# Graph layer on one core: each strip of node features is loaded where it is normalised, into two buffers, in place of two strips ahead into three

## The chip, the core and the metric

The kernel runs on one NeuronCore of a Trainium2 chip. The metric is device time of one launch in microseconds (us), the median of several runs; three runs of the kernel before gave 2588.91, 2590.05 and 2590.2 us, so the median is 2590.05 us. One execution was also recorded by the hardware profiler; everything called "the trace" or "the profile" below is that execution.

The engines are PE (matrix products), DVE (vector work), ACT (activation functions and copies), POOL (here almost only indirect DMAs) and SP (issues of DMAs). Each takes its instructions strictly in the order in which the program gives them. DMAs are issued by SP, ACT and POOL and are carried out by 16 DMA engines that all issuers share.

## What is computed

One layer of a graph network over 12,500 nodes with 64 features and 212,500 edges sorted by destination:

```
h = relu(layernorm(x))                        # 12500 x 64
edge_in = concat([h[src], h[dst], weight])    # 212500 x 129
e = silu(silu(edge_in @ eW1 + eb1) @ eW2 + eb2)
agg = segment_sum(e, src, 12500)              # 12500 x 128
out = x + silu(concat([h, agg]) @ nW1 + nb1) @ nW2 + nb2
```

## The kernel before

The product of `edge_in` with `eW1` is split: the part of `h[src]` and the part of `h[dst]` are products of nodes, made once for each node and written to two tables in DRAM, `ta` and `tb`.

**Strips.** Node number n belongs to bucket n mod 100; there are 100 buckets of 125 nodes. The node features are taken in strips of 12 buckets (`CH` = 12): eight strips of 12 and a ninth of 4, numbered 0 to 8 here. A strip goes through three steps. It is loaded into a buffer `xs` of 128 x 12 x 64 (function `loaded`, two DMAs of SP on line 570, one for 112 partitions and one for 13). It is normalised in place by `norm`, called by `normed`: DVE sums it (L532, L533) and centres it (L535), ACT squares (L536), DVE sums the squares (L539, L540), ACT takes the root (L541), DVE inverts and scales (L543, L544). Then `products` handles four buckets at a time: PE turns them (L551) and multiplies (L180), ACT copies out (L555, L183, L591, L597), DVE splits the rows into three bf16 parts (L593, L599), and SP writes the results to `hd`, `tb` and `ta` (L586, L594, L601).

**Blocks.** The edges are taken in 208 blocks of 1024. For a block s, `count` makes a one-hot of the edges' buckets (L306, L307), a running count by a scan in three pieces (L317) and a product (L322). `send` takes the rank of each edge from PE (L341), makes destination rows `to` on DVE (L361), the products of the `tb` window with PE (L349), copies them to `qs` on ACT (L356, L365), and POOL scatters them with eight indirect DMAs (L370) into a queue `q` in DRAM. SP loads what a block needs: `bc` and `bb` (L265, L267), the window `win` (L281) and the edge weights `pick` (L292). There are 11 chunks of blocks, each with a queue; while one chunk is sent, ACT issues the fills of the next chunk's queue with zeros (L100, up to 1.6 MB in one DMA).

**Steps.** When a chunk is sent, its queue is read back (`qt`, L415, with rows of `ta`, `a`, L420), and a pipeline of steps (L438 to L516) finishes the edges and adds them up by bucket. Steps of chunk c run among the sends of chunk c+1.

**Order.** PE, DVE, ACT and SP run in the order in which the program emits instructions. The strips' work is a generator, `feed`, that is advanced a few pieces at a time between the pieces of `send_all`: four at each piece while chunk 0 is sent and for some pieces after it, then two at each hook of the steps' loop. `groups` makes the list of the strips' pieces, and `turns` keeps up to three of them going in turn, one piece of each in a round. In the kernel before, strips 0 and 1 are loaded first, then strip 0 is normalised; from then on strip i+2 is loaded ahead of the products of strip i, and strip i+1 is normalised after the first products of strip i. With three buffers strip i uses buffer i mod 3.

Of the kernel before, what the change touches and what calls it, by code (L numbers as in the profile page):

```python
# [28 lines left out]
F32 = mybir.dt.float32  # L29
# [9 lines left out]
P = 128  # L39
# [7 lines left out]
G = 4  # L47
# [12 lines left out]
def tile_gnn(ctx: ExitStack, tc: tile.TileContext, x, src, dst, ew, eW1, eb1, eW2, eb2, nW1, nb1, nW2, nb2, out):  # L60
    nc = tc.nc
    N, D = x.shape
# [44 lines left out]
    CH = 12  # L107
# [64 lines left out]
    def product(s, hr, ps, tag, to):  # L172

        abs_ = []
        for a in range(2):

            half = slice(a * D, (a + 1) * D)
            ab = ps.tile([P, G // 2, H], F32, name="ab", tag=tag)
            for i in range(G // 2):
                nc.tensor.matmul(ab[:, i], hr[half, i, :], w1[half, s, :], start=True, stop=True)  # L180
            abs_.append(ab)
        for a in range(2):
            nc.scalar.copy(to.rearrange("l (i a) h -> l a i h", a=2)[:, a], abs_[a])  # L183
# [7 lines left out]
    for win in wins:  # L191
        nc.vector.memset(win, 0.0)
        for a in range(2):
            for i, row in enumerate((w1d, eb1b)):
                at = a * HB + WL + i
# [43 lines left out]
    with ExitStack() as work:  # L239
# [287 lines left out]
        def norm(xs, n):  # L527

            xs = xs[:, :n, :]
            wide = [P, n, D]  # L530
            mean = fp.tile([P, NE], F32, name="mean")[:, :n]
            nc.vector.tensor_reduce(mean, xs, AX.X, OP.add)  # L532
            nc.vector.tensor_scalar(mean, mean, 1.0 / D, None, op0=OP.mult)  # L533
            cen = fp1.tile([P, NE, D], F32, name="cen")[:, :n]
            nc.vector.tensor_tensor(cen, xs, mean[:, :, None].to_broadcast(wide), op=OP.subtract)  # L535
            nc.scalar.activation(xs, cen, AF.Square)  # L536
            yield
            var = fp.tile([P, NE], F32, name="var")[:, :n]
            nc.vector.tensor_reduce(var, xs, AX.X, OP.add)  # L539
            nc.vector.tensor_scalar(var, var, 1.0 / D, EPS, op0=OP.mult, op1=OP.add)  # L540
            nc.scalar.activation(var, var, AF.Sqrt)  # L541
            yield
            nc.vector.reciprocal(var, var)  # L543
            nc.vector.scalar_tensor_tensor(xs, cen, 0.0, var[:, :, None].to_broadcast(wide), op0=OP.max, op1=OP.mult)  # L544
            yield

        def turned(xs, g):

            ht = mm.tile([P, G // 2, P], F32, name="ht", tag="mm")
            for i in range(G // 2):  # L550
                nc.tensor.transpose(  # L551
                    ht[:, i, :], xs[:, g + 2 * i : g + 2 * i + 2, :].rearrange("p j d -> p (j d)"), ident
                )
            hr = fp.tile([P, G // 2, P], F32, name="hr")
            nc.scalar.copy(hr, ht)  # L555
            return hr
# [8 lines left out]
            nc.sync.dma_start(tb0.rearrange("(p j) f -> p j f", j=NE)[:, g : g + G, :], got)  # L565
            yield

        def loaded(b0, n, xs):
            for part_ in (slice(0, 112), slice(112, L)):
                nc.sync.dma_start(xs[part_, :n, :], x_rows[part_, b0 : b0 + n, :])  # L570
            yield

        def normed(b0, n, xs):
            yield from norm(xs, n)
            yield
            ready.add(b0)

        def products(b0, g, xs):

            assert b0 in ready  # L580
            b = b0 + g
            hr = turned(xs, g)
            yield
            rows_a = fp.tile([P, G, H], F32, name="rows_a")
            product(0, hr, mm, "mm", rows_a)
            nc.sync.dma_start(hd[:, b // 2 : (b + G) // 2, :], hr)  # L586
            yield
            got = fp.tile([P, G, H], F32, name="got")
            product(1, hr, mm, "mm", got)
            parts = fp.tile([P, G, 3, H], BF16, name="parts")  # L590
            nc.scalar.copy(parts[:, :, 0, :], rows_a)  # L591
            yield
            nc.vector.tensor_tensor(rows_a, rows_a, parts[:, :, 0, :], op=OP.subtract)  # L593
            nc.sync.dma_start(tb_buckets[:, b : b + G, :], got)  # L594
            done_b.append(b // G)
            yield
            nc.scalar.copy(parts[:, :, 1, :], rows_a)  # L597
            yield
            nc.vector.tensor_tensor(parts[:, :, 2, :], rows_a, parts[:, :, 1, :], op=OP.subtract)  # L599
            yield  # L600
            nc.sync.dma_start(ta_buckets[:, b : b + G, :], parts.rearrange("p b s f -> p b (s f)"))  # L601
            done_a.append(b // G)
            yield
# [84 lines left out]
        def groups():  # L688

            starts = list(range(0, NB, CH))  # L690
            size = lambda b0: min(CH, NB - b0)
            of = [(b0, size(b0), xss[i % len(xss)]) for i, b0 in enumerate(starts)]
            todo = [loaded(*of[0]), loaded(*of[1]), normed(*of[0])]
            for i, b0 in enumerate(starts):
                if i + 2 < len(starts):
                    todo.append((b0, loaded(*of[i + 2])))
                todo += [(b0, products(b0, g, of[i][2])) for g in range(0, size(b0), G)]
                if i + 1 < len(starts):
                    todo.insert(len(todo) - size(b0) // G + 1, normed(*of[i + 1]))
            return todo  # L700

        done_a, done_b, ready = [], [], set()
        feeding = ExitStack()
        fp = feeding.enter_context(tc.tile_pool(name="fp", bufs=3, side="right"))
        fp1 = feeding.enter_context(tc.tile_pool(name="fp1", bufs=1, side="right"))
        xss = [fp1.tile([P, CH, D], F32, name=f"xs{i}") for i in range(3)]
        for xs in xss:
            nc.gpsimd.memset(xs, 0.0)

# [2 lines left out]
        with tc.tile_pool(name="lists", bufs=1, side="right") as lp:  # L712
# [4 lines left out]
            f, sf, t = (lp.tile([NP, PAIR], F32, name=n) for n in ("f", "sf", "t"))  # L717
# [25 lines left out]
            for _ in counting:  # L743
                pass
            feed = itertools.chain(checks(), turns(groups(), 3))
            for _ in send_all(0):
                for _ in range(4):
# [30 lines left out]
        at = 0  # L778
        for k in range(first, len(steps) + 2):
            for s in turn:  # L780
# [17 lines left out]
                else:  # L798
                    f, ahead = s
# [152 lines left out]
```

## Time and profile before

| quantity | value |
|---|---|
| median of three runs | 2590.05 us |
| the profiled execution, time and span | 2590.2 us, 2588.4 us |
| PE, DVE, ACT, POOL busy, share of the span | 85%, 79%, 48%, 67% |
| mean granted clock of PE | 0.926 |
| first and last indirect DMA of POOL (1661 of them) | 63.7 us, ended 2340.1 us |
| loads of strips (L570), first and last issue | 64.9 us, 246.9 us |
| sums of strips (L532), first and last start | 77.2 us, 290.8 us |
| fills of the second and third queue that lie among them, issue | 62.45, 91.49, 102.61, 152.59, 165.93, 184.05 and 202.49 us |

Times in the trace count from the start of the span. The strips are handled in the first eighth of the span, while chunks 0 and 1 are sent. "Busy" for POOL counts the execution of an indirect DMA and not the time of some 0.3 us between two of them, which the profile names "issue". What a wait is put down to is inferred by the profile from the semaphore that came last.

### The profile page before, as it was taken

The numbers are of one execution on the slowest core, as the hardware profiler recorded it, in microseconds if no ns is written. First come the engines' busy times: TensorE is split into PE (matmuls) and PEld (weight loads), VectorE is DVE, ScalarE is ACT, GpSimd is POOL, SyncE is SP. The second block draws the span as 40 slices with busy tenths as digits, with TensorE's granted clock in tenths as the row PEclk, the third lists the DMA queues.
The fourth block names the chain that finished last, engine by engine and source line by source line (L and its number), as shares of the span: only waits on it lengthen the run. The fifth ranks groups of instructions, "written<-read, shape, count | busy, mean of one in ns | idle before, by whom it ended". The sixth has DMA issues, their size and how long they took to land.

```text
span 2588.4 us, 60017 instructions
## 1 busy us (share of the span) xinstructions
PE 2205.0 (85%) x21814; PEld 2041.8 (79%) x21814; DVE 2034.8 (79%) x3464; ACT 1246.9 (48%) x2687; POOL 1736.8 (67%) x1729
## 2 busy tenths in 40 slices
PE   2456777988998998999899799889889999997997
PEld 1345667977987987888788799889879889996996
DVE  5877987987987887888788799879879889973442
ACT  2344634544554554555455455445545455553443
POOL 3675777777777777777677777777767777772000
PEclk7556888998999999999999899999989999998999
DMA  8787778669768767866966877786696667655441
GB/s 202 216 246 263 254 234 271 217 204 269 237 210 247 252 219 227 267 216 218 272 227 211 240 248 237 220 260 228 211 274 228 215 203 235 230 169 174 166 150 54
DMA packets 257977, 577.23 MB, mean 223 GB/s; under 512 B 51202, under 2 KB 110580, under 8 KB 257469
## 3 DMA queue, kind: packets, MB, share of 16 engines
q1 hardware_dynamic: 185096, 384.91, 45.7%
q0 software_dynamic: 54144, 123.04, 13.1%
q10 hardware_dynamic: 18434, 65.37, 11.4%
q8 instruction: 175, 2.87, 0.5%
q14 instruction: 128, 1.04, 0.1%
HBM read 361.44 MB, written 211.67 MB: 221 GB/s over the span
## 4 chain that ended last, share of the span: by engine, by line
PE 40%; DMA 23%; DVE 13%; POOL 7%; issue 6%; ACT 2%; SPq 1%; DVEq 0%; ACTq 0%; POOLq 0%
DMA q<-qs,to 14%; PE seg L505 10%; PE p L491 9%; POOL q L370 7%; PE pt L459 7%; PE pt L452 5%; DVE misc L317 5%; PE qp L349 4%; PE lr L438 3%; DMA bc<-rows 2%; DVE oneT L443 2%; DMA bb<-rows 2%; DVE one L472 2%; DMA pick<-in_edge_weight_dram 2%; DVE own L322 2%
## 5 line engine op out<-in xcount | busy, mean ns | idle before, releaser
L370 POOL DMA_INDIRECT q<-qs,to x1661 | 1697.4, 1022 | 602.7 <-issue 397.5
L463 ACT ACTIVATE e<-pt 128x512 f32<-128x512 f32 x525 | 313.7, 598 | 835.8 <-PE pt L459 769.6
L505 PE MATMUL seg<-one,e 128*128 128x125 f32 x4200 | 581.4, 282 | 54.7 <-DVE aggT L516 42.5
L491 PE MATMUL p<-w,e 128*128 128x128 f32 x4200 | 587.2, 284 | 5.3 <-ACT p L485 5.3
L317 DVE TENSOR_TENSOR_SCAN misc<-oh,misc 100x342 f32<-100x342 f16 (+1 forms) x623 | 579.7, 930 | 9.3 <-PE misc L341 1.2
L505 PEld LDWEIGHTS seg<-one,e 128*128 128x128 f32 x4200 | 524.4, 196 | 68.5 <-ACT p L485 27.7
L491 PEld LDWEIGHTS p<-w,e 128*128 128x128 f32 x4200 | 527.9, 197 | 31.0 <-issue 8.4
L443 DVE TENSOR_SCALAR oneT<-lr,part 125x512 bf16<-125x512 f32 x525 | 390.8, 744 | 111.1 <-PE lr L438 109.0
L459 PE MATMUL pt<-oneT,a 125*128 125x256 bf16 (+1 forms) x3300 | 443.0, 273 | 0.1
L452 PE MATMUL pt<-ident,qt 128*128 128x128 f32 x2100 | 332.0, 282 | 73.4 <-DVE oneT L443 73.4
L356 ACT COPY qs<-qp 128x512 f32<-128x512 f32 x416 | 229.2, 587 | 320.3 <-PE qp L349 225.7
L472 DVE TENSOR_TENSOR one<-nodes,qt 128x500 f32<-128x500 f32 x525 | 351.7, 670 | 0.7 <-PE seg L505 0.5
L459 PEld LDWEIGHTS <-a 125*128 125x128 bf16 x3300 | 318.7, 100 | 35.5 <-issue 1.0
L322 DVE TENSOR_TENSOR own<-misc,oh 100x342 f16<-100x342 f32 (+1 forms) x623 | 320.0, 514 | 21.6
L495 ACT ACTIVATE e<-p 128x512 f32<-128x512 f32 x525 | 314.1, 598 | 18.6 <-PE p L491 18.0
L485 ACT COPY p<-b2f 128x512 f32<-128x512 f32 x525 | 312.5, 595 | 0.1
L349 PE MATMUL qp<-win,pick 50*128 50x128 f32 x3322 | 260.7, 299 | 60.6 <-DMA pick<-in_edge_weight_dram 34.5
L349 PEld LDWEIGHTS qp<-win,pick 50*128 50x128 f32 x3322 | 220.4, 200 | 92.9 <-issue 71.5
L452 PEld LDWEIGHTS pt<-ident,qt 128*128 128x128 f32 x2100 | 228.3, 144 | 79.0 <-DVE oneT L443 76.3
L516 DVE TENSOR_TENSOR aggT<-aggT,seg 128x500 f32<-128x500 f32 x250 | 166.9, 667 | 94.2 <-PE seg L505 93.9
L438 PE MATMUL lr<-identb,qt 128*125 128x128 bf16 x2100 | 213.3, 225 | 30.6 <-DMA qt<-q 25.3
L438 PEld LDWEIGHTS <-qt 128*125 128x125 bf16 x2100 | 186.4, 139 | 42.1 <-DMA qt<-q 31.5
(121 smaller groups left out, 1086.3 us busy)
## 6 DMA issues: line engine op xcount, KB each, us to landing
qt<-q SPq DMA_DIRECT2D x250, 576.0 KB
a<-ta SPq DMA_DIRECT2D x275, 384.0 KB
q<-zeros ACTq DMA_DIRECT2D x30, 1638.0 KB
bb<-rows SPq DMA_DIRECT2D x208, 224.0 KB
bc<-rows SPq DMA_DIRECT2D x208, 128.0 KB
q<-qs,to POOLq DMA_INDIRECT x1661
win<-tb SPq DMA_DIRECT2D x416, 24.0 KB
ta<-parts SPq DMA_DIRECT2D x25, 384.0 KB
```

What stands on the lines that cost most here:

```text
L317: nc.vector.tensor_tensor_scan(run[:, :m], oh[:, cols], nil.to_broadcast([NB, m]), carry.get(c, -1.0), op0=OP.add, op1=OP.add)
L322: nc.vector.tensor_tensor(own[:, cols], run[:, :m], oh[:, cols], op=OP.mult)
L349: nc.tensor.matmul(qps[a][:, t, :], pick[half, t * P : (t + 1) * P], win[half, :], start=True, stop=True)
L370: i = nc.gpsimd.indirect_dma_start(out=q[:], out_offset=bass.IndirectOffsetOnAxis(ap=to[:k, t : t + 1], axis=0), in_=qs[:k, t - t0, :], in ...
L438: nc.tensor.matmul(lr[:L, t, :], loc[:, at : at + 1].to_broadcast([P, L]), identb, start=True, stop=True)
L443: nc.vector.tensor_scalar(oneT, st[k].pop("lr")[:L], part1[:L, :], None, op0=OP.is_equal)
L452: nc.tensor.matmul(pt[:, t, :], qt[:, j, :H], ident, is_transpose=True, start=t == 0, stop=False, skip_group_check=True)
L459: nc.tensor.matmul(pt[:, cols, :], a3[:L, b, i, :], oneT[:, cols, :], start=False, stop=i == 2, skip_group_check=True)
L472: nc.vector.tensor_tensor(one.rearrange("p (b j) l -> p b j l", j=n), nodes1[:, None, None, :].to_broadcast(wide), loc[:, tiles[0][1] : ti ...
L491: nc.tensor.matmul(p2[:, t, :], e1[:, t, :], w2, start=False, stop=t == G - 1, skip_group_check=True)
L495: nc.scalar.activation(e2, p2, AF.Silu)
L505: nc.tensor.matmul(item[2][:, b, :], e2[:, t, :], one[:, t, :], start=j < G, stop=j >= G * (n - 1))
```

## The change

The function `loaded` goes; its two DMAs become the first piece of `normed`, one round ahead of the first sum. The list of `groups` has no loads of its own any more: strip 0 is loaded and normalised first, and the load of strip i+1 stands with its normalisation, after the first products of strip i. There are two buffers, and strip i uses buffer i mod 2. One `memset` of a buffer on POOL goes. The number of DMAs and of pieces is the same. Scan, product, rank and PSUM are not touched.

```diff
-        def loaded(b0, n, xs):
+        def normed(b0, n, xs):
             for part_ in (slice(0, 112), slice(112, L)):
                 nc.sync.dma_start(xs[part_, :n, :], x_rows[part_, b0 : b0 + n, :])
             yield
-
-        def normed(b0, n, xs):
             yield from norm(xs, n)
             yield
             ready.add(b0)
@@
             starts = list(range(0, NB, CH))
             size = lambda b0: min(CH, NB - b0)
-            of = [(b0, size(b0), xss[i % len(xss)]) for i, b0 in enumerate(starts)]
-            todo = [loaded(*of[0]), loaded(*of[1]), normed(*of[0])]
+            todo = [normed(0, size(0), xss[0])]
             for i, b0 in enumerate(starts):
-                if i + 2 < len(starts):
-                    todo.append((b0, loaded(*of[i + 2])))
-                todo += [(b0, products(b0, g, of[i][2])) for g in range(0, size(b0), G)]
+                todo += [(b0, products(b0, g, xss[i % 2])) for g in range(0, size(b0), G)]
                 if i + 1 < len(starts):
-                    todo.insert(len(todo) - size(b0) // G + 1, normed(*of[i + 1]))
+                    at = len(todo) - size(b0) // G + 1
+                    todo.insert(at, normed(starts[i + 1], size(starts[i + 1]), xss[(i + 1) % 2]))
             return todo
@@
-        xss = [fp1.tile([P, CH, D], F32, name=f"xs{i}") for i in range(3)]
+        xss = [fp1.tile([P, CH, D], F32, name=f"xs{i}") for i in range(2)]
         for xs in xss:
             nc.gpsimd.memset(xs, 0.0)
```

## The prediction, made before the changed kernel ran

> **What bounds the kernel now.** I read the page first, then busy time by stretch, then POOL's instructions in order of time, then those of DVE, ACT and SP around the strips.
>
> ```profile
> POOL 3675777777777777777677777777767777772000
> PEclk7556888998999999999999899999989999998999
> L370 POOL DMA_INDIRECT q<-qs,to x1661 | 1697.4, 1022 | 602.7 <-issue 397.5
> ...
> 60.00:160.00 100.00, 65.06 (x63) 0.50 0.76 222
> 160.00:235.00 75.00, 42.92 (x42) 0.57 0.83 259
> 235.00:1000.00 765.00, 579.87 (x565) 0.94 0.74 236
> 1000.00:2340.00 1340.00, 1009.49 (x993) 0.97 0.72 230
> ...
>   DVE to L361: 149.3, 81
>   ACT qs L356: 87.4, 62
> ```
>
> The first two lines are busy tenths of POOL and PE's granted clock in 40 slices; the third is POOL's indirect DMAs; the next four are POOL's busy time on L370 by stretch; the last two are who waited for L370 (us, times). POOL looks 67% busy and PE 85%, but an indirect DMA executes 0.97 us and the next begins 0.30 us later, the 397.5 us of "issue". From 235 to 2340 us there are 1558 in 2105 us, one in 1.35 us, and its gaps over 0.45 us add up to 48.5 us there, none longer than 3.1. POOL never rests in that stretch, and DVE's L361 and ACT's L356 wait for it. After its last send, 2340.1 us, comes a tail of 248.3 us on the last chunk. So the end is POOL's start, plus POOL's stretch, plus a fixed tail, and what the change does is read from where POOL is kept waiting:
>
> ```profile
> 83.64 1.22 POOL L370 DMA_INDIRECT q<-qs,to  x1 [9.92 <-DVE var L543]
> ...
> 97.01 0.96 POOL L370 DMA_INDIRECT q<-qs,to  x1 [3.01 <-ACT qs L365]
> ...
> 188.30 0.96 POOL L370 DMA_INDIRECT q<-qs,to  x1 [4.17 <-ACT got L183]
> ...
> 208.25 0.97 POOL L370 DMA_INDIRECT q<-qs,to  x1 [9.61 <-ACT hr L555]
> ...
> 223.48 0.97 POOL L370 DMA_INDIRECT q<-qs,to  x1 [4.71 <-ACT hr L555]
> ```
>
> Columns: start, duration, instruction, idle before it and its releaser. All large gaps lie between 73 and 235 us, among the strips. I also took, for each block, how long its `to` and first `qs` were ready before POOL began it (its lead). It is 0.3 to 0.7 us for blocks 1 to 4, 1.6 to 5.0 for 5 to 9, 0.3 for 10 to 13, 1.0 for 14, 5.3, 3.6, 4.6, 6.6, 6.1 for 15 to 19, and 13 to 31 from block 23 (348 us) to the end. A delay of DVE beyond the lead delays POOL, hence the end, one for one; behind 348 us the leads would carry POOL's shift to the end unchanged.
>
> **The change, part by part.** Before, a strip's sum found its data: of nine L532 one waited for a DMA.
>
> ```profile
> 77.16 0.95 DVE L532 TENSOR_REDUCE mean<-xs 128x12 f32<-128x768 f32 x1 [2.82 <-DMA xs<-in_x_dram]
> ...
> 112.08 1.04 SPq L570 DMA_DIRECT2D xs<-in_x_dram  x2
> ...
> 131.44 0.95 DVE L532 TENSOR_REDUCE mean<-xs 128x12 f32<-128x768 f32 x1
> ```
>
> The load of 112.08 is used at 131.44. In the changed program's instruction order a load and its L532 have 28 DVE instructions between them for strip 0, then 3, 5, 0, 3, 4, 0, 0, 0 for strips 1 to 8 (before: 28 to 67). DVE, in order, must now sit out what is left of the load, with counts (L317, L322) and `to` behind it; POOL waits for `to`, and PE's L341 for the counts.
>
> A load's length: first issue to both halves landed, by the landing records, 4.6 us (112.08 to 116.70), 5.0, 5.0, 4.1 and 3.8; I take 4.6. Where a zero fill (9.6 to 13.5 us from issue to landing) runs ahead of it, 12.2 us: strip 0, 64.86 to 77.04.
>
> A page bears on the length. The Trainium skill (SBUF — State Buffer, "The DMA setup-cost knee") gives 2 us plus bytes by 436 GB/s: an estimate of 2.9 us for a strip's 384,000 bytes. These rows are 1 to 2 us longer, with bc, bb and writes in flight beside them; with the page's figure the sum would be about 13 us instead of the one below.
>
> *Strip 0.* One strip is loaded in place of two, so its halves may land up to 1.6 us sooner (the first landed at 75.48). But block 1's `to`, which ended POOL's 9.92 us gap, now stands behind L543 and L544: sqrt wait 0.4, 0.22 and 0.96, some 1.6. Together +0.5 (-1.5 to +2).
>
> *Strip 1.* SP issues it behind hd<-hr (85.22 + 0.36), so 85.6, landing 90.2; L532 started at 86.86. Stall 3.3, less 1.3 of DVE's wait for the square, which other work now fills: +2 on a block with lead 0.3 (0 to 4.3).
>
> *Strip 2.* Its load stands on SP behind block 4's pick, which SP issued at 111.40 (two fills, of 91.49 and 102.61, stretch SP's issues to 2 us), behind hd and tb, 0.4 each. With the +2 that is some 115, landing 119. Its L532 stands ahead of block 5's L306, 112.03 before, so 113: stall 6 ahead of block 4's `to`, lead 0.3. +6 (2 if SP comes sooner, 9 if a fill still runs).
>
> *Strip 3.* The load follows ta<-parts and pick, 1 us behind DVE's L599; DVE has L317, L322, L361 (1.6) before the sum. Stall 4.0, against leads of 4.7 on the next blocks: 0 (to 3).
>
> *Strip 4.* A fill of the next queue (152.59 before) is issued just ahead, so 12.2 in place of 4.6: stall 10. Leads are 3 to 4.5, and ACT stood 7.3 us beside that fill in any case (until L183 at 166.57). But ACT's next fill now stands behind this strip's L536 and L541, which wait for DVE, so the fills that cost POOL its gaps are strung out. +5 (-4 if they fall in better places, as POOL loses 21 us in gaps from 160 to 235; +12 if the stall and a fill add).
>
> *Strip 5.* Load behind tb<-got; DVE has 2.3 us of work: stall 2, on a block without lead. +1.5 (0 to 5).
>
> *Strip 6.* Load behind ta<-parts, which waits for the very L599 ahead of the sum: 0.4 + 4.6 = 5.0 of stall ahead of block 13's `to`, lead 0.3; in such stretches leads grew by about 1 us a block (0.3 to 5.3 from block 13 to 15), so I take 1 off. +4 (0 to 5.5).
>
> *Strip 7.* Stall 3.8, leads 3.6 and 4.6 behind it: +0.5 (to 4). *Strip 8* is a third as large: stall 2, lead 6.1: 0 (to 1).
>
> *At nothing:* one POOL memset, 0.76 us, covered by POOL's wait of 23.7 us for the first `qs`; without it, +0.8 saved. The reuse of a buffer two strips on makes SP wait for PE's last L551 on it, emitted about a block earlier; were it late, pick (L292) queues behind it, and PE's L349 waits for pick (18.4 us in two waits already). SP has the same 18 loads, moved back past hd, tb and ta writes.
>
> Sum: 0.5 + 2 + 6 + 0 + 5 + 1.5 + 4 + 0.5 + 0 = 19.5 us; the bounds add up to -3.5 and +45.8. Span 2588.4 + 19.5 = 2607.9, and with the 1.8 us around the span 2609.7 beside the profiled run's 2590.2. The median was 0.15 lower: 2609.5.
>
> A rule speaks against this. The Trainium skill (Trainium Kernel Development and Optimization, "Best Practices") asks for double buffers so that DMA overlaps compute, and two buffers remain here, which by itself would give 0 us. But the trace's overlap came from when a load was issued, some 19 us ahead at 112.08, and no row says that a third buffer was what gave it.
>
> **The rivals.**
> *No change that shows (within 5 us).* POOL's eight `qs` tiles and the fill stretch absorb the stalls: for it, DVE idles 32 us of 75 between 160 and 235; against it, leads of 0.3 at blocks 2, 4 and 13, ahead of which three stalls fall. Strips 2 and 6 would have to fall to their low ends and strip 4 to 0: 19.5 - 4 - 4 - 5 = 6.5, or less with strips 1 and 5 covered: about 2593. 10%.
> *Faster.* One mechanism: the four fills between 152 and 212 us, shifted against SP's loads, no longer hold up ACT and `bc`/`bb`. POOL's 21 us of gaps there would have to shrink by more than the other strips' 14.5 us plus 5.2, so by 19.7; with all of it gone the time is 2590 + 14.5 - 21 = 2583.5, and lower where other strips fall to their low ends too. Nothing in the order moves a fill away from the loads. 6%.
> *Much slower.* Most strips meet a fill or a slow SP queue and leads don't refill: the upper bounds of strips 2, 4, 5 and 6, 9 + 12 + 5 + 5.5, with 2.5 for strips 0 and 1 and 4 for 3 and 7: 38, so 2628. 15%.
> *The change isn't what its words say.* The words that came with the change speak of counts, ranks and PSUM; the scan (L317) and the product (L322) are the same instructions in both programs, so nothing is to be had from them, whichever case holds.
>
> **How the numbers follow.** My forecast has 69%, with 2598 to 2622 of its own. The range leaves out the faster case, half of the "no change" and a third of the "much slower": 2591 to 2630. A run can tell 0.2%, 5.2 us, from no change: slower is 69 + 15 = 84%, same 10%, faster 6%.
>
> **What would show it.** DVE's L532 waits for "DMA xs", some 30 us over eight or nine waits (2.8 in one before); POOL's first sends of blocks 2, 4 and 13 come 2, 8 and 16 to 20 us later than 97.0, 118.8 and 236.5; POOL's gaps between 63 and 240 grow by the whole difference; from 350 us on POOL keeps one in 1.35 us, and the tail stays near 248 us. I am wrong if L532 waits and POOL doesn't move, if POOL's shift shrinks after 350 us, or if the fill stretch changes by more than the stalls.

## The result, and the profile after

The changed kernel takes 2633.12 us (median of four runs, 2626.99 to 2636.84); the kernel before took 2590.12 us beside it (four runs, 2588.91 to 2591.15). The ratio is 1.0164, with a 95% interval of 1.0143 to 1.0185: slower by 43 us. The profiled execution is the one of 2626.99 us, the fastest of the four, with a span of 2625.2 us, 36.8 us longer than the span of before. So the traces explain 36.8 us.

From the page of after: the length of the span, POOL's busy tenths and the clock granted to PE in 40 slices, and POOL's indirect DMAs (busy us, mean ns of one, then the idle time just before them).

```profile
span 2625.2 us, 60018 instructions
...
POOL 3554677777777777777777777767777777772000
PEclk9856877998998999899899999989989999998999
...
L370 POOL DMA_INDIRECT q<-qs,to x1661 | 1705.4, 1027 | 633.5 <-issue 400.6
```

The number and the mean length of POOL's DMAs are those of before; only the idle time grew (602.7 before), and the lower digits stand in slices 2 to 5, among the strips. POOL's busy time by stretch in after (the columns are the stretch, its length, busy time with the count, PE's clock, the share of the DMA engines and GB/s):

```profile
60.00:160.00 100.00, 57.86 (x56) 0.76 0.67 191
160.00:235.00 75.00, 33.98 (x33) 0.56 0.76 214
235.00:1000.00 765.00, 568.75 (x554) 0.90 0.75 235
...
1000.00:2370.00 1370.00, 1038.58 (x1014) 0.97 0.72 230
```

POOL sent 16 fewer from 60 to 235 us than before (89 instead of 105) and 11 fewer from 235 to 1000. At one in 1.35 us these 27 are 36 us, about the difference of the spans. From 1000 us on the cadence is the old one: 1370 us by 1014 is 1.35 us. The last send ended at 2378.0 us, 37.9 later than before, and the tail is 247.2 us (248.3 before). The whole loss is made among the strips and carried to the end.

What each sum of a strip waited for, DVE's instructions in order of time in after (start, duration, instruction, and in brackets the idle time ahead of it and its releaser):

```profile
75.62 0.95 DVE L532 TENSOR_REDUCE mean<-xs 128x12 f32<-128x768 f32 x1 [2.06 <-DMA xs<-in_x_dram]
...
86.95 0.95 DVE L532 TENSOR_REDUCE mean<-xs 128x12 f32<-128x768 f32 x1 [1.05 <-DMA xs<-in_x_dram]
...
117.64 0.95 DVE L532 TENSOR_REDUCE mean<-xs 128x12 f32<-128x768 f32 x1 [7.54 <-DMA xs<-in_x_dram]
...
148.39 0.95 DVE L532 TENSOR_REDUCE mean<-xs 128x12 f32<-128x768 f32 x1 [5.55 <-DMA xs<-in_x_dram]
...
182.63 0.95 DVE L532 TENSOR_REDUCE mean<-xs 128x12 f32<-128x768 f32 x1 [11.14 <-DMA xs<-in_x_dram]
...
219.64 0.95 DVE L532 TENSOR_REDUCE mean<-xs 128x12 f32<-128x768 f32 x1 [14.53 <-DMA xs<-in_x_dram]
...
259.92 0.95 DVE L532 TENSOR_REDUCE mean<-xs 128x12 f32<-128x768 f32 x1 [6.53 <-DMA xs<-in_x_dram]
...
295.99 0.95 DVE L532 TENSOR_REDUCE mean<-xs 128x12 f32<-128x768 f32 x1 [4.76 <-DMA xs<-in_x_dram]
...
330.28 0.42 DVE L532 TENSOR_REDUCE mean<-xs 128x4 f32<-128x256 f32 x1 [3.31 <-DMA xs<-in_x_dram]
```

All nine wait, 56.5 us together, where one of nine waited 2.8 us before. Five of the longest gaps of POOL in after (behind that ahead of block 1, which before had too), same columns, each behind one of these waits:

```profile
125.14 1.22 POOL L370 DMA_INDIRECT q<-qs,to  x1 [8.62 <-ACT qs L365]
...
186.34 0.97 POOL L370 DMA_INDIRECT q<-qs,to  x1 [9.10 <-DVE misc L317]
...
223.08 0.97 POOL L370 DMA_INDIRECT q<-qs,to  x1 [12.83 <-ACT qs L365]
...
264.95 0.97 POOL L370 DMA_INDIRECT q<-qs,to  x1 [6.59 <-ACT hr L555]
...
306.19 0.97 POOL L370 DMA_INDIRECT q<-qs,to  x1 [5.83 <-ACT qs L365]
```

The releaser named is the last in the chain (a count, a copy to `qs`), never the load: what is late is DVE, and each of these sends starts 3 to 11 us after a sum that came late. POOL's gaps over 0.6 us from its second send to 330 us add up to 76.7 us; they were 35.5 before.

### The profile page after: what moved, and what is told of

Its sections match the earlier page's. It is cut to its first block, busy times and chain, and to the rows that moved or that the text cites. A ratio compares the mean times of both kernels' runs of the same rounds, so it can differ in the third digit from the quotient of the medians.

```text
span 2625.2 us, 60018 instructions
## 1 busy us (share of the span) xinstructions
PE 2206.0 (84%) x21814; PEld 2046.5 (78%) x21814; DVE 2032.2 (77%) x3464; ACT 1248.6 (48%) x2687; POOL 1743.9 (66%) x1728
## 3 DMA queue, kind: packets, MB, share of 16 engines
q10 hardware_dynamic: 18434, 65.37, 11.1%
## 4 chain that ended last, share of the span: by engine, by line
PE 45%; DMA 23%; DVE 15%; POOL 7%; issue 6%; ACT 2%; SPq 2%; DVEq 0%; ACTq 0%; POOLq 0%
DMA q<-qs,to 15%; PE seg L505 10%; PE p L491 10%; PE pt L459 8%; POOL q L370 7%; PE pt L452 5%; DVE misc L317 5%; PE qp L349 4%; PE lr L438 3%; DVE oneT L443 2%; DVE one L472 2%; DMA xs<-in_x_dram 2%; DVE own L322 1%; DMA bb<-rows 1%; DVE aggT L516 1%
## 5 line engine op out<-in xcount | busy, mean ns | idle before, releaser
L505 PE MATMUL seg<-one,e 128*128 128x125 f32 x4200 | 582.8, 283 | 44.2 <-DVE aggT L516 36.5
L459 PEld LDWEIGHTS <-a 125*128 125x128 bf16 x3300 | 320.1, 100 | 35.7 <-issue 1.2
```

The source lines that it names most:

```text
L459: nc.tensor.matmul(pt[:, cols, :], a3[:L, b, i, :], oneT[:, cols, :], start=False, stop=i == 2, skip_group_check=True)
L505: nc.tensor.matmul(item[2][:, b, :], e2[:, t, :], one[:, t, :], start=j < G, stop=j >= G * (n - 1))
```

## The experiments

The theory: DVE sits out each load in order, and POOL gets the delay nearly one for one, so the time goes with the wait at L532. The rivals: the number of buffers matters (a load waits for its buffer to come free); or the new order by itself (where the loads and norms fall among the zero fills) matters, wait or not. In the readings below, "shift" is how much later POOL's first send of a block starts than in the program it is compared with.

### What part of the change costs the time

The new order with three buffers (strip i also uses buffer i mod 3):

```diff
-        xss = [fp1.tile([P, CH, D], F32, name=f"xs{i}") for i in range(2)]
+        xss = [fp1.tile([P, CH, D], F32, name=f"xs{i}") for i in range(3)]
```

> The changed kernel with a third buffer given back, loads still one round ahead of their sums. A: nothing changes, 2627 to 2637 us, waits at L532 of 50 to 60 us. B: 2590 to 2600 us. C: as A.

Measured: 2632.12 us, ratio 1.0136 (1.0119 to 1.0154); this interval and that of after overlap. The sums wait as in after, and the gaps of POOL stand at the same blocks.

Two buffers, but strip i+1 is loaded ahead of the products of strip i:

```diff
+                if 1 <= i < len(starts) - 1:
+                    todo.append((b0, loaded(*of[i + 1])))
```

> The kernel before with two buffers, strip i+1 loaded ahead of the products of strip i, where strip i+2 was loaded. Between a load and its sum L532 stand 28, 34, 6, 7, 5, 14, 17, 16, 8 DVE instructions for strips 0 to 8 (after: 28, 3, 5, 0, 3, 4, 0, 0, 0). Theory A (what costs is DVE sitting at L532 until the load lands, in order, with counts and POOL's sends behind it): some 3 to 9 us of DVE work now cover a load of 4.6 us, so waits at L532 of 5 to 20 us in place of 56.5, and 2593 to 2612 us. Rival B (the third buffer is what counts): as after, 2627 to 2637 us. Rival C (the pieces of the strips stand elsewhere among fills and blocks, the wait is only a sign of it): no reason to be near before, anywhere from 2590 to 2637 us with no tie to the L532 waits.

Measured: 2598.29 us, ratio 1.0016 (0.9999 to 1.0033); POOL's shift from before is 2.7 us at block 24. The waits of DVE between 60 and 340 us in these two kernels (us in all, times, longest), three buffers first:

```profile
DVE mean L532 <- DMA xs<-in_x_dram: 53.8, 9, 15.4
```

```profile
DVE mean L532 <- DMA xs<-in_x_dram: 19.8, 3, 8.8
```

A third buffer doesn't take the waits away, and two buffers with earlier loads take most of them. The buffers don't set the cost; the moment of the load does.

The order of after, but every load goes to a tile that nothing reads:

```diff
-                nc.sync.dma_start(xs[part_, :n, :], x_rows[part_, b0 : b0 + n, :])
+                nc.sync.dma_start(unread[part_, :n, :], x_rows[part_, b0 : b0 + n, :])
```

> The changed kernel, whose strip loads go to a tile that nothing reads; the normalisation works on what the two buffers held, so the strips' values are not those of x, and L532 has no load to wait for. Instructions and DMAs stand in the changed kernel's order. A: 2588 to 2600 us, no wait at L532, POOL's gaps from 63 to 350 us near the 35 us of before. C: as after, 2625 to 2637 us, with gaps of some 75 us. B says nothing of it.

Measured: 2592.72 us, ratio 0.9994 (0.9984 to 1.0004). The longest waits of DVE between 60 and 340 us in this kernel have no load among them:

```profile
DVE rows_a L591 <- ACT parts L589: 30.0, 14, 6.2
DVE parts L597 <- ACT parts L595: 7.4, 3, 4.1
DVE oneT L443 <- PE lr L438: 5.7, 1, 5.7
```

Same DMAs, same instructions, same order, and the 43 us are gone. So the order among the fills costs nothing by itself, and the wait for the data is the whole cost. This kernel is also the right one to count from, since it differs from after only in the tile that the loads go to, and so in the waits:

| strip | wait at L532 in after | block | shift there, from the order with nothing read | added by this strip |
|---|---|---|---|---|
| 0 and 1 | 3.1 | 3 | +1.5 | 1.5 |
| 2 | 7.5 | 4 | +9.2 | 7.7 |
| 3 | 5.5 | 8 | +11.8 | 2.6 |
| 4 | 11.1 | 10 | +21.4 | 9.6 |
| 5 | 14.5 | 12 | +26.8 | 5.4 |
| 6 | 6.5 | 14 | +32.4 | 5.6 |
| 7 | 4.8 | 17 | +39.5 | 7.1 |
| 8 | 3.3 | 24 | +40.3 | 0.8 |

So 56.5 us of wait add 40.3 to POOL's shift. The order with nothing read is itself 4.5 us ahead of before at block 24, hence the 35.7 us between before and after there. Two things in these traces stay unexplained. Strips 2 and 7 add more than their own waits; of strip 7's 7.1 us, 1.3 stood at block 15 already, ahead of its wait. And a small lead isn't kept: at the last send the order with nothing read is 4.2 us behind before, so that after is then 33.7 us behind it, not 40.3.

### Which strips cost it

In the kernel before, only some strips are loaded next to their sum:

```diff
+        NEAR = (4, 5)
@@
+            if b0 // CH in NEAR:
+                yield from loaded(b0, n, xs)
@@
-                if i + 2 < len(starts):
+                if i + 2 < len(starts) and i + 2 not in NEAR:
```

> The kernel before with strips 4 and 5 alone loaded one round ahead of their sums, the others as before, three buffers. These two fall among the fills of 152 to 212 us. A, as the trace of after has it (POOL's shift rose from 10 to 26 us between blocks 8 and 12): +10 to +18 us, 2600 to 2608 us. A as predicted (+5 and +1.5): 2595 to 2598 us. If the fills are strung out only because POOL and DVE have lost their lead at strips 2 and 3: +0 to +5 us.

Measured: 2610.54 us, ratio 1.006 (1.0044 to 1.0077); waits 29.9 us in three, shift from before 12.2 at block 23. The same with `NEAR = (1, 2, 3)`:

> The kernel before with strips 1, 2 and 3 alone loaded one round ahead of their sums. As predicted, 2 + 6 + 0 = +8 us over before. As the trace of after has it (POOL's shift 10 us at block 8, of which strip 1 none): +9 to +11 us if the fills of 152 to 212 us pass the shift on whole; +4 to +7 us if the gaps there take part of it back, as in the kernel with two buffers and loads ahead (8 us at block 4, 5 at block 12).

Measured: 2599.51 us, ratio 1.0031 (1.002 to 1.0042); waits 15.4 us in four, shift 8.2 at block 4 and 4.8 at block 24. With `NEAR = (6, 7, 8)`:

> The kernel before with strips 6, 7 and 8 alone loaded one round ahead of their sums. As predicted, 4 + 0.5 + 0 = +4.5 us. As the trace of after has it (shift 24.6 at block 12, 35 from block 16 on): +9 to +12 us. With leads of before in place at strip 7 (3.6 to 6 us) and not used up: +5 to +7 us.

Measured: 2601.26 us, ratio 1.0032 (1.0016 to 1.0047); waits 15.0 us in four, shift 2.7 at block 13, 7.7 at block 16, 8.8 at block 24: strip 7 adds 5 here too. The three parts add up to 0.31 + 0.60 + 0.32 = 1.23%, or 32 us, against 1.64% for after and 1.36% with three buffers. In the parts the loads of strips 3 and 5 were issued 14.6 and 21.0 us ahead of their sums, against 5.1 and 5.4 in after, so the parts don't cover the whole change.

The other way round, the order of after with only the named strips read, counted from the order with nothing read:

```diff
+            to_ = xs if b0 // CH in (7,) else unread
@@
-                nc.sync.dma_start(xs[part_, :n, :], x_rows[part_, b0 : b0 + n, :])
+                nc.sync.dma_start(to_[part_, :n, :], x_rows[part_, b0 : b0 + n, :])
```

> The program after, but only strip 7's load is read from its buffer (all others go into a buffer that nothing reads, and the norm works on what the buffers hold); a chip where the kernel before takes some 2590 us is wanted. One L532 wait of about 5 us. If the leads of POOL on blocks 16 and 17 (3.6 and 4.6 us before) cover a lone strip, POOL's shift from before at block 18 stays as in the program with no strip read (about -4.5 us) and the time is 2590 to 2594. If a stall goes into POOL whether or not an earlier one has used the leads up, the shift there is 4 to 6 us higher and the time 2596 to 2600.

Measured: 2598.84 us, ratio 1.0029 (1.0013 to 1.0045). The sum of strip 7 and POOL's gap behind it in this kernel:

```profile
263.18 0.95 DVE L532 TENSOR_REDUCE mean<-xs 128x12 f32<-128x768 f32 x1 [5.12 <-DMA xs<-in_x_dram]
```

```profile
273.17 0.97 POOL L370 DMA_INDIRECT q<-qs,to  x1 [6.62 <-ACT qs L365]
```

POOL's shift steps from 0.5 at block 15 to 6.5 at block 16 and 6.8 at block 18. A lone strip 7 is not covered at all, with no earlier stall to have used up a lead: in the new order with nothing read, the leads of blocks 15, 16 and 17 are 0.3, 0.7 and 2.2 us; in before they were 5.3, 3.6 and 4.6.

With strips 4 and 5 read (`in (4, 5)`):

> The program after, but only the loads of strips 4 and 5 are read. Two L532 waits, of about 14 and 5 us, 19 together. If the strips among the fills cost what the program after showed between blocks 8 and 12 (14 us), whatever came ahead of them, the time is 2604 to 2608 and POOL's shift at block 12 is 14 us above that of the program with no strip read. If the earlier strips (2 and 3) had used up the leads of blocks 5 to 9, the cost here is about 10 us or less, 2600 to 2603.

Measured: 2603.97 us, ratio 1.0046 (1.0026 to 1.0065); two waits, 26.0 us (10.7 and 15.3); shift 8.0 at block 9, 12.8 at block 12, 13.5 at block 24. In after the two strips added 15.0. So what they cost depends little on the strips ahead of them, and about half of their wait doesn't show in POOL's shift.

Six runs of such kernels fell in sessions in which the kernel before itself took 3457.39 and 3573.14 us, with PE's clock between 0.82 and 0.85 in the records, and don't bear on the question at the usual speed; they are the following four (strip 3 alone, strip 7 alone, strips 6 and 7, strips 4 and 5) and, later, strip 3 alone again and strips 2 and 3.

> The changed kernel's order, with all strips but strip 3 loaded into a tile that nothing reads (their values are not those of x), so that only strip 3's sum waits. To be read against the run in which no strip waits (2592.72 us). If a lead covers a stall, as predicted: 0 to +2 us, and POOL's shift at block 8 within 1 us. If the stall passes to POOL in spite of the lead: +3 to +5 us. If only the lead used up by strip 2 made it cost: 0 to +1 us.

> The same with strip 7 alone waiting. If a lead of 3.6 to 5 us covers the stall: 0 to +2 us. If the stall of 5.5 us and the norm behind it in order pass to POOL: +4 to +6 us.

> The same with strips 6 and 7 waiting. If strip 7 costs because strip 6 has used up the lead: +9 to +11 us, and more than 4 us above strip 7 alone plus 4. If each costs what it costs alone: 4 us more than strip 7 alone.

> The same with strips 4 and 5 alone waiting. As predicted, 5 + 1.5 = +6.5 us. If the whole wait of some 20 us (14.5 for strip 4) passes to POOL less the lead of 3 to 5 us: +13 to +17 us. If POOL's gaps among the fills take most of it: 0 to +5 us.

Measured, in that order: 3470.17, 3462.24, 3474.25 and 3482.82 us; ratios 1.0036 (1.0003 to 1.0069), 1.0019 (0.9973 to 1.0065), 0.9991 (0.9943 to 1.004) and 1.0046 (1.0008 to 1.0084).

> The program after, but only strip 3's load is read. In the program with no strip read POOL's leads on blocks 6 to 8 are 6.0, 3.9 and 5.1 us. One L532 wait of 4 to 5 us. If those leads cover a lone strip, POOL's shift at blocks 7 and 8 stays within 1 us of the program with no strip read (-2.8, -1.6), and the time is 2590 to 2594. If a stall goes into POOL whatever lead there is, the shift there is 3 to 5 us higher and the time 2596 to 2599.

> The program after, but only the loads of strips 2 and 3 are read. Two L532 waits, about 10 and 5 us. POOL's shift at block 4 some 9 us above the program with no strip read (strip 2, in front of a block with no lead). If strip 2's stall uses up the leads of blocks 5 to 7, strip 3 adds 2 to 4 us more at blocks 7 and 8 (12 us above), as in the program after, though it costs nothing alone; if leads do not matter, it adds the same as in the run with strip 3 alone. Time 2600 to 2606.

Measured: 3578.44 and 3574.37 us; ratios 1.0019 (0.9989 to 1.0048) and 1.001 (0.9977 to 1.0043). The leads in these traces are 0.3 us at most blocks, so they don't show whether a lead of 4 to 6 us would have covered a lone strip 3. That stays open.

### The fills' length, and the start

If the long fills (1.6 MB in one DMA) make the loads late, cutting them should shrink the difference. First the kernel before with fills of 0.47 MB, then the kernel after with them; the edit is the same:

```diff
-            zeros_left = list(fill(c + 1, nc.scalar, 7)) if c + 1 < len(chunks) else []
+            zeros_left = list(fill(c + 1, nc.scalar, 2)) if c + 1 < len(chunks) else []
```

> The kernel before with the zero fills cut into 13 DMAs of up to 0.47 MB a queue in place of 4 of up to 1.6 MB. Control for the next run. If the fills hold up POOL between 160 and 235 us only by the length of one DMA, -5 to -20 us against before; if by their bytes, 0 +- 5 us; with 9 more issues a queue on ACT, up to +5 us.

> The changed kernel with the same smaller fills. To be read against the kernel before with smaller fills. If what the changed kernel loses at strips 4 and 5 (16 us of POOL's shift) comes of a load that lands behind a long fill: the two differ by 25 to 33 us, with waits at L532 of 35 to 45 us. If it does not depend on the length of a fill: by 38 to 45 us, waits of 50 to 60 us.

Measured: 2542.84 us, ratio 0.9802 (0.9782 to 0.9822), and 2584.86 us, ratio 0.9968 (0.9952 to 0.9984), both against the kernel before. The difference between them is 42.0 us, as with long fills. The waits at L532 are 40.4 us in the second, and POOL's shift between the two is 36.5 us at block 24: these shorter waits pass almost whole. So the length of a fill isn't what the change costs. The first of the two is the fastest kernel of this study, by its interval 1.8 to 2.2% faster than the kernel before.

Two kernels load strips 0 and 1 at the very start of the program, to close POOL's gap of 9.92 us ahead of block 1 (DVE, not POOL, then sets the buffers to zero); the second also takes the checks of the feed in turn with the first strip. The edit of the first:

```diff
-            todo = [loaded(*of[0]), loaded(*of[1]), normed(*of[0])]
+            todo = [normed(*of[0])]
@@
+            for i in range(2):
+                for _ in loaded(i * CH, CH, xss[i]):
+                    pass
```

> The kernel before, with strips 0 and 1 loaded at the start of the program on SP, behind the list of sources, and the buffers set to zero by DVE. The wait of 2.8 us at strip 0's sum goes, and with it part of POOL's gap of 9.9 us ahead of block 1. The theory that DVE's waits for strips pass to the end one for one: -2 to -4 us against before. If the loads at the start delay the lists (SP in order): 0 to +4 us.

> The same with the scaling of the other chunks' rows (checks, L679 and L670 to L673, 13 us of DVE) taken in turn with the first strip's work in place of ahead of it, so that strip 0 is normalised ahead of block 0's rows. POOL's gap of 9.9 us ahead of block 1 should shrink to 1 to 5 us, against up to 3 us lost ahead of its first send: -4 to -9 us against before, if the shift is kept through the fills; -2 to +3 us if the gaps among the fills take it back.

Measured: 2596.02 us, ratio 1.0009 (0.9992 to 1.0026), and 2592.8 us, ratio 1.0002 (0.9987 to 1.0018). No sum of a strip waits for its load in the first; the gap ahead of block 1 is 8.47 us, then 5.43 in the second. What was won there was lost again behind: POOL's first sends of block 24 come 2.7 and 5.9 us earlier than before, its last ones 11.2 and 1.6 later. Here a gap closed at the start was worth nothing by itself, while the delay of after was carried to the end; what makes the difference, the traces don't show.

## Why the prediction was right and wrong

**The bound was read rightly.** POOL's chain of sends sets the end, and its shift at block 24 reaches the last send within 3 us (35.7 and 37.9). The cadence and the tail stayed, as said. POOL's gaps grew by 41.2 us, which is the difference of the spans and 4 us more.

**The mechanism was right.** The sums wait, and the kernel with nothing read, which takes the waits away and nothing else, is back at the time of before. POOL's first sends of blocks 2, 4 and 13 were to come 2, 8 and 16 to 20 us later; they came -1.6, +6.3 and +28.5. The waits at L532 were to be some 30 us and were 56.5. That the number of buffers is neutral was right too. The Trainium skill asks to double-buffer, so that DMA overlaps compute (Trainium Kernel Development and Optimization, "Best Practices"). Here two buffers overlapped only what was issued ahead: 1.0016 with the load a strip ahead, 1.0164 without, both with two buffers.

**The size was off by 17 us of span: 19.5 predicted, 36.8 measured** (and by 24 in the median, since the profiled run of after was its fastest). Two steps failed: the leads that were counted as cover, and the length of strip 5's stall. Between the sum of 19.5 and the table's 40.3 lie 20.8 us: strips 3 and 7 make 9.2 of them, strips 4 and 5 make 8.5, the rest 3.1. By the prediction's own terms, each against the table above:

- *Strips 0 and 1*, +2.5: 1.5. SP issued the load of strip 1 at 83.0 us, not 85.6. Against before, block 3 even came 2.0 us earlier.
- *Strip 2*, +6: block 4's first send came at 125.14 against 118.8, +6.3; right.
- *Strip 3*, 0: 2.6. *Strip 7*, +0.5: 7.1. The stalls were predicted as 4.0 and 3.8 and measured as 5.5 and 4.8, near enough. What failed is the step "Stall 3.8, leads 3.6 and 4.6 behind it", and for strip 3 "against leads of 4.7 on the next blocks: 0". These leads were read from the trace of before and taken as belonging to the blocks. They belong to that order: with the norms at new places, blocks 15 to 17 had 0.3 to 2.2 us with nothing read, and the lone strip 7 cost 6 to 7 us. For strip 3 the leads were there in the new order (6.0 and 3.9 at blocks 6 and 7 with nothing read), and half of its wait was covered; that strip 2 had used up the rest wasn't shown.
- *Strips 4 and 5*, +6.5: 15.0. Strip 4's stall was right (10 predicted, 11.1 measured), but nearly all of it reached POOL, where leads of 3 to 4.5 and the time that ACT stands beside a fill had been counted as cover. Strip 5 was mis-sized at "DVE has 2.3 us of work: stall 2"; it waited 14.5 us. SP around that load in after (start, duration, instruction):

```profile
202.54 2.01 SPq L267 DMA_DIRECT2D bb<-rows  x1
206.64 4.70 SPq L281 DMA_DIRECT2D win<-tb  x2
211.46 2.35 SPq L592 DMA_DIRECT2D tb<-got  x1
214.24 1.22 SPq L570 DMA_DIRECT2D xs<-in_x_dram  x2
```

  A fill was running (200.5 to 216.5 us, behind one from 189.4 to 201.7), and each of the four issues ahead of the load took SP 2.0 to 2.4 us ("x2" are two issues), where the median of L281 over the run is 0.34. DVE had nothing left from 205.1 us on, so 9 of the 14.5 us are the queue ahead of the load and 5.4 the load. The prediction had counted such slow issues for strip 2 and forgot them here. Only some 5 us of this wait were added to POOL's shift (strip 5's row in the table): in the order with nothing read POOL waits 15.4 us for ACT at block 11 in any case.
- *Strip 6*, +4: 5.6. The 1 us taken off for a lead growing "by about 1 us a block" doesn't fit the rows named for it, 5.0 us in two blocks; the cost came out higher, not lower. *Strip 8*, 0: 0.8. *At nothing*: no cost shows; three buffers gave nearly the same waits (53.8 us).

The rival "much slower", whose words were that "most strips meet a fill or a slow SP queue and leads don't refill", described what happened: its 38 us of shift are close to the table's 40.3, though the 2628 us that it gave are 5 below the median. It was worth more than 15%.

**The length of a load** was taken as 4.6 us. The loads of after took, from first issue to both landed, 3.8 (strip 1), 4.2, 5.1, 5.4, 5.4, 5.5 and 6.0 us, and 11.8 and 10.9 for strips 0 and 4 behind a fill. The Trainium skill's figures (SBUF — State Buffer, "The DMA setup-cost knee") give an estimate of 2.9 us; the measurement decides.

## What to carry to other kernels

A load placed right in front of its reader can cost its whole latency plus the DMA queue ahead of it at every such place, even if there is a free buffer (here 56.5 us of wait, of which 40.3 counted); move the issue, not the buffer count. Where an engine that works in order waits, assume that the saturated engine behind it gets the wait, and take slack off only when it is known to exist in the changed order: slack read from the old trace belongs to the old order. To size such a loss, run the new order with the data dependence removed; the difference by block then gives the cost of each wait.

## What was not expected of the hardware

**With shorter fills POOL ends 40 us earlier.** With the zero fills cut from 1.6 MB to 0.47 MB a DMA, and the same bytes, the kernel before is 2% faster. The edit also spreads the fills: 13 DMAs a queue, one or two at a block, instead of 4 at the first four blocks. Length and spreading weren't tried apart. (PE's clock was 0.943 in that record against 0.926; the kernel with nothing read had 0.941 at the time of before, so the clock doesn't make the 2%.) The waits of POOL, in the kernel before and then in the one with short fills:

```profile
POOL q L370 <- DMA q<-qs,to: 62.7, 90, 3.1
...
POOL q L370 <- ACT hr L555: 14.9, 4, 9.6
```

```profile
POOL q L370 <- issue: 404.4, 1325, 0.7
...
POOL q L370 <- ACT qs L365: 52.1, 51, 21.0
POOL q L370 <- DMA q<-qs,to: 22.0, 72, 0.3
```

The waits of POOL for its own earlier sends fall by 40.7 us, and none is longer than 0.3 us any more. POOL is 13 us ahead at block 24 and gains some 2 to 4 us more in every 20 blocks, 40.3 at block 200. Why these fills leave POOL's sends alone, the traces don't show.

**The same kernel can take a third longer.** In two sessions, on two chips, the kernel before took 3457.39 and 3573.14 us; one of these chips had run it in 2591.26 us in another session. The page of the run with strip 3 alone in the later one:

```profile
PE 2790.3 (78%) x21814; PEld 2466.0 (69%) x21814; DVE 2046.9 (57%) x3464; ACT 1259.2 (35%) x2687; POOL 1715.2 (48%) x1728
...
POOL 3655555555545454554545544545545555445100
PEclk9757677888878778887878887877878888889999
```

DVE, ACT and POOL are as busy as ever in us, and PE takes 2790.3 us against 2206.0 in after, at a granted clock of 0.816 instead of 0.928. PE's busy time is 1.26 times that of after and its clock 1.14 times lower, so the granted clock alone doesn't account for it. POOL was no longer the engine that never rests: its busy digits are 4 and 5 nearly all along, and it waited 895.1 us for ACT's copies to `qs`, which follow products of PE. There the stalls of the strips made ratios between 0.9991 and 1.0046, and four of the six intervals hold 1. What made the sessions slow, no trace here shows.
